# A gated graph network followed by graph attention: another order of the work ahead of the first block

## The chip, the cores and the metric

The kernel runs on one core of a Trainium2 chip. The core has five engines that run side by side, each working through its own list of instructions in order and waiting on semaphores for the others: TensorE (PE in the profile, with weight loads shown as PEld), VectorE (DVE), ScalarE (ACT), GpSimd (POOL) and SyncE (SP, which here only issues transfers). The metric is the device time of one execution in microseconds, lower is better; the figure for a kernel is the median of its runs.

## The reference

There are 64 graphs of 256 nodes with 256 features. Layer 0 is a gated graph network of three steps with one recurrent cell, layer 1 is graph attention. Each adds its result to its input and normalises.

```
A = (adj != 0)
h = x
for i in range(3):
    m = einsum('bnd,de->bne', h, weight[i])
    aggr = einsum('bst,bsd->btd', A, m)
    h = gru_cell(aggr, h, w_ih, w_hh, b_ih, b_hh)
x = layernorm(x + h)

Wh = x @ W;  s1 = Wh @ a[:256];  s2 = Wh @ a[256:]
e = leaky_relu(s1[:, :, None] + s2[:, None, :], 0.2)
attn = softmax(where(adj > 0, e, -9e15), axis=2)
out = layernorm(x + attn @ Wh)
```

## The kernel before

Two graphs form a pair, and there are 32 pairs. A pair goes through three recurrent blocks (one for each layer i of the network), then through its attention. The blocks of different pairs are interleaved: (0,0), (1,0), (0,1), (2,0), (1,1) and so on, so that the side work of one block lies beside the matmuls of another. "(p,i)" stands for block i of pair p in what follows.

The weight of a step is folded into the input weight of the cell: since aggr @ w_ih.T = (A.T h) weight[i] w_ih.T, the kernel forms weight[i] w_ih.T once for each i ("fold", L234) and aggregates h itself (L439). The large products are made in a reduced format from three pieces of each factor: an upper piece H (ScalarE, L132), a lower piece L (L135, or L149 for weights) and a cross piece D (L138). So `hH`, `hL`, `hD` are the pieces of the state, `aH`, `aL`, `aD` those of the aggregate, `whhH/L/D` and `wc0H/L/D` to `wc2H/L/D` those of the weights. `cut_weight` (L140) makes the three pieces of a weight out of a PSUM bank: upper on ScalarE, a remainder `cut` on VectorE, its scaling on GpSimd (L149), the cross piece on VectorE. While the program's clock is negative, the remainder's buffer is one of three of the tag "n"; afterwards it is the single buffer "wh".

A block's `gates` (L456) runs four products for each of the two halves e of the state: r (6 pairs of matmuls on two PSUM banks, `pga` and `pgb`), n (3 pairs on the state alone), z (6), t (3 on the aggregate alone). All of them are line L468. An evacuation (L473, L475, L477), a nonlinearity (L486) and blending (L494 to L507) follow each product on ScalarE, VectorE and GpSimd.

The order of the work is written out by hand. `at(t, step)` and `after(dt, step)` put a step into a heap by its tick; `tick()` advances the program's clock and emits all steps that are due, those of one tick in the order in which they were entered. `gates` calls `tick()` between parts of its products. Ticks order instructions when the program is built; they are not time on the chip. `front` (L385) enters the preparation of a block with a `pace`: ticks of turning x to the transposed state (L280), its split into `hi` and `lo` (L405, L135), aggregation (L439), pieces of the aggregate, and in a second tuple the pieces hH, hL, hD of the state.

Eight PSUM banks serve everything (`bank`, L106). A new bank is one whose earlier reader has been emitted, so a matmul that opens a bank waits for the engine that reads that earlier content.

Ahead of block (0,0) the kernel turns w_ih (`rows_inp`, tiles `rows_aH`, `rows_aL`) and w_hh (`rows_hid`, tiles `rows_hH`, `rows_hL`) on TensorE (L219), cuts w_hh, folds weight[0] (`square_T` at L222 turns it, L238 multiplies), makes the 0/1 matrix A of the first pair (`ones`, L380), and aggregates. The folds of weight[1] and weight[2] and `attention_rows` (L242) are entered for later ticks and are emitted inside the first blocks. `attention_rows` forms two extra columns of W, W a1 and W a2 (L247, copied by L249), and takes the column means off (a tile `mean` filled with 1/256 at L251, the matmul L254, the subtraction L256); the results are used only much later, by the first attention (L589).

Of the kernel before, what the change touches and what calls it, by code (L numbers as in the profile page):

```python
# [9 lines left out]
F32 = mybir.dt.float32  # L10
# [9 lines left out]
P = 128  # L20
# [7 lines left out]
def kernel(  # L28
# [37 lines left out]
    nc = tc.nc  # L66
    B, N, D = x.shape
# [25 lines left out]
    def after(dt, step):  # L93
        at(clock[0] + dt, step)
# [5 lines left out]
    def tick(n=1):  # L100
        for _ in range(n):
            clock[0] += 1
            run_due()


    def bank(name):  # L106
        return psum.tile([P, 512], F32, tag="bank", name=name)
# [3 lines left out]
    def evacuate(dst, src):  # L111
        copies[0] += 1
        if copies[0] % 2:
            nc.scalar.copy(dst, src)
        else:
            nc.vector.tensor_copy(dst, src)
# [55 lines left out]
    def load_adj(p):  # L172
        if p < NP:
            a_sb = loaded_adj[p] = io.tile([P, G, C, N], I32, tag="adj", name=f"adj_{p}")
            nc.sync.dma_start(a_sb, adj[p * G:(p + 1) * G].rearrange("g (c p) n -> p g c n", p=P))
# [34 lines left out]
    def wih(e, o0, o1):  # L210

        return (wihT if o1 <= 512 else wihT2)[:, e, o0 % 512:o0 % 512 + o1 - o0]

    def rows_T(src, use):
        o0, o1, t = src
        for c in range(C):
            pt = bank("pw")
            for o in range(o1 - o0):
                nc.tensor.transpose(pt[:, o * P:(o + 1) * P], t[:, o, c * P:(c + 1) * P], ident)  # L219
            use(c, o0 * P, o1 * P, pt[:, :(o1 - o0) * P])  # L220

    def square_T(src, name):  # L222
        pt = bank("pw")
        for e in range(C):
            for d in range(C):
                nc.tensor.transpose(pt[:, (e * C + d) * P:(e * C + d + 1) * P],
                                    src[:, d, e * P:(e + 1) * P], ident)
        dst = work.tile([P, GN], F32, tag="z", name=name)
        nc.scalar.copy(dst, pt)
        return dst.rearrange("p (e d) -> p e d", e=C)  # L230
# [3 lines left out]
    def fold(i, wT, d, parts=PARTS):  # L234
        for o0, o1 in parts:
            pt = bank("pw")
            for e in range(C):
                nc.tensor.matmul(pt[:, :o1 - o0], wT[:, e, d * P:(d + 1) * P], wih(e, o0, o1),  # L238
                                 start=(e == 0), stop=(e == C - 1))
            cut_weight([t[:, d, o0:o1] for t in wc[i]], pt[:, :o1 - o0], f"{i}_{d}_{o0}")  # L240

    def attention_rows():  # L242
        gwT = square_T(gw, "gwT")
        for d in range(C):
            pt = bank("pw")
            for f in range(C):
                nc.tensor.matmul(pt[:, :2], gwT[:, f, d * P:(d + 1) * P], a_w[:, :, f],  # L247
                                 start=(f == 0), stop=(f == C - 1))
            nc.vector.tensor_copy(gw[:, d, D:], pt[:, :2])  # L249
        mean = late.tile([P, C, GN], F32, tag="vT", name="mean")[:, 0, :P]  # L250
        nc.vector.memset(mean, 1.0 / D)  # L251
        pt = bank("pw")[:, :D + 2]
        for d in range(C):
            nc.tensor.matmul(pt, mean, gw[:, d, :], start=(d == 0), stop=(d == C - 1))  # L254
        for d in range(C):
            nc.vector.tensor_sub(gw[:, d, :], gw[:, d, :], pt)  # L256


    class Pair:
# [112 lines left out]
    def begin(p):  # L372
        s = pairs.setdefault(p, Pair())
        s.hT = work.tile([P, C, GN], F32, tag="hT", name=f"hT_{p}", bufs=4)

    def ones(p):
        s = pairs[p]
        s.adj = loaded_adj.pop(p)
        s.A = work.tile([P, G, C, N], F32R, tag="A", name=f"A_{p}", bufs=3)
        nc.vector.tensor_scalar(s.A, s.adj, 0.0, None, op0=ALU.not_equal)  # L380
# [469 lines left out]
    def rows_hid(part):  # L850
        rows_T(part, lambda c, o0, o1, pt: cut_weight([t[:, c, o0:o1] for t in whh], pt, f"h{c}_{o0}"))

    def rows_inp(part):
        rows_T(part, lambda c, o0, o1, pt: evacuate(wih(c, o0, o1), pt))
    begin(0)
    take_x(0)
    front(0, 0, clock[0] + 1, ((0, 1, 2, 9, 11, 12), (7, 8, 13)))
    tick(2)
    rows_inp(wi_n[0])
    tick()  # L860
    rows_hid(wh_n[0])
    tick()
    rows_inp(wi_n[1])
    tick()
    rows_hid(wh_n[1])
    wT = square_T(w_n[0], "wT_0")
    nc.vector.tensor_add(b_sum, bi, bh)
    tick()
    ones(0)
    load_adj(1)  # L870
    tick()
    for parts in PARTS:
        for d in range(C):
            fold(0, wT, d, (parts,))
            tick(2)
    tick(10)
    load_x(1)
    clock[0] = 0
    wTs = {}

    def start_fold(i):
        wTs[i] = square_T(w_n[i], f"wT_{i}")
    for i in range(1, L):
        after(8 * i - 7, lambda i=i: start_fold(i))
        for d in range(C):
            after(8 * i - 5 + 3 * d, lambda i=i, d=d: fold(i, wTs[i], d))
    after(8 * L - 7, attention_rows)

    for n, (p, i) in enumerate(blocks):
        if n + 1 < len(blocks):  # L890
# [59 lines left out]
```

## Time and profile before

| what | value |
|---|---|
| median of three runs | 2091.16 us (2088.38 to 2096.8) |
| the profiled execution | 2091.86 us |
| its span, first to last instruction | 2090.0 us |
| TensorE busy in the span | 2052.3 us (98%) |
| TensorE busy in 0 to 28 us | 17.55 us |
| TensorE busy in 28 to 62 us | 34.00 us |
| TensorE busy in 62 to 78 us | 13.27 us, granted clock 0.89 |
| TensorE busy in 78 to 178 us | 100.00 us, granted clock 1.00 |
| mean granted clock over the span | 0.996 |

The profile page gives the busy time of each engine, and the chain of waits that ended last. Other views of the same trace give the busy time in any stretch, the instructions in order of time with the idle time ahead of each and what ended it, and the waits of one engine summed by what ended them. "Busy" for TensorE contains a modelled end of each matmul, so start-to-start distances are the better measure of its pace.

### The profile page before, as it was taken

To read this page: it belongs to the slowest core of one execution; us is meant where nothing else is said; L and a number is where in the kernel's file an instruction comes from. 1 tells how busy PE (TensorE), PEld (TensorE's weight loads), DVE (VectorE), ACT (ScalarE), POOL (GpSimd) and SP (SyncE) were. 2 spreads that over 40 slices of the span, in tenths; PEclk is the share of its full clock that TensorE was granted. 3 is DMA by queue.
4 is the path that set the end of the run, shared out by engine and by line. 5 is a ranking of instruction groups with operands and counts; after the bars stand their busy time and mean duration, and the time that the engine had idled before them with its cause. 6 is when DMAs were issued, how large, how long until landed. Compare 5 with 4: busy or idle time off the path is not lost.

```text
span 2090.0 us, 31381 instructions
## 1 busy us (share of the span) xinstructions
PE 2052.3 (98%) x9892; PEld 1726.0 (83%) x9892; DVE 1780.5 (85%) x2886; ACT 1655.3 (79%) x3015; POOL 1604.8 (77%) x1114
## 2 busy tenths in 40 slices
PE   8999999999999999999999999999999999999996
PEld 5788888888888888888888888888888888888885
DVE  5666778898888899888998988998888998988887
ACT  4566787888887888888888887888888888888775
POOL 6777777777877787878777877787878787878763
PEclk9999999999999999999999999999999999999998
DMA  4111235665666665665665666665766665666321
GB/s 131 31 41 41 72 88 114 141 141 117 136 138 135 141 137 121 136 136 137 140 136 124 136 137 137 137 138 123 134 138 139 134 141 123 138 136 137 61 61 61
DMA packets 531621, 247.98 MB, mean 119 GB/s; under 512 B 359616, under 2 KB 523200, under 8 KB 531456
## 3 DMA queue, kind: packets, MB, share of 16 engines
q1 hardware_dynamic: 529664, 244.14, 53.1%
q8 instruction: 79, 1.29, 0.3%
q10 hardware_dynamic: 1616, 1.57, 0.2%
q14 instruction: 86, 0.70, 0.1%
q0 software_dynamic: 176, 0.27, 0.1%
HBM read 69.74 MB, written 33.55 MB: 49 GB/s over the span
## 4 chain that ended last, share of the span: by engine, by line
PE 89%; DVE 3%; ACT 3%; issue 2%; POOL 1%; DMA 1%; SPq 0%; POOLq 0%; ACTq 0%; DVEq 0%
PE pga L468 46%; PE pgb L468 23%; PE pa L439 8%; PE pwh L589 5%; PE po L673 5%; DVE lo L135 1%; PE s L608 1%; PE pt L369 1%; ACT sc L636 1%; DMA rows_hH<-in_L_gnn_w_hh_dram 0%; PE po L796 0%; ACT L636 0%; PE pw L238 0%; ACT n L475 0%; DMA second<-v 0%
## 5 line engine op out<-in xcount | busy, mean ns | idle before, releaser
L494 POOL TENSOR_TENSOR t<-hT,n 128x512 f32<-128x512 f32 x192 | 263.0, 1370 | 191.6 <-ACT n L486 191.3
L500 POOL TENSOR_TENSOR n<-n,r 128x512 f32<-128x512 f32 x192 | 316.5, 1648 | 81.8 <-ACT r L486 42.6
L504 POOL TENSOR_TENSOR n<-n,t 128x512 f32<-128x512 f32 x192 | 282.7, 1472 | 122.7 <-DVE t L477 116.0
L468 PE MATMUL pga<-hH,whhH_whh 128*128 128x512 f32 x1152 | 370.5, 403 | 0.0
L468 PE MATMUL pgb<-hD,whhD_whh 128*128 128x512 f32 x1152 | 356.8, 391 | 1.4 <-DVE hD L138 1.4
L468 PE MATMUL pga<-hL,whhL_whh 128*128 128x512 f32 x1152 | 356.7, 391 | 0.4 <-POOL hL L135 0.4
L495 POOL TENSOR_TENSOR t<-t,z 128x512 f32<-128x512 f32 x192 | 271.4, 1414 | 15.1
L135 POOL TENSOR_TENSOR hL<-hT,hH 128x1024 fp32r<-128x1024 f32 x96 | 255.5, 2661 | 9.0 <-ACT hH L132 9.0
L468 PEld LDWEIGHTS pgb<-hD,whhD_whh 128*128 128x128 f32 x1152 | 216.2, 188 | 49.2 <-DVE hD L138 1.7
L468 PEld LDWEIGHTS pga<-hL,whhL_whh 128*128 128x128 f32 x1152 | 216.2, 188 | 47.8 <-POOL hL L135 0.8
L468 PEld LDWEIGHTS pga<-hH,whhH_whh 128*128 128x128 f32 x1152 | 207.5, 188 | 34.1
L473 ACT ACTIVATE r<-pga 128x512 f32<-128x512 f32 x192 | 114.1, 594 | 109.1 <-PE pga L468 79.6
L439 PE MATMUL pa<-A,lo 128*128 128x256 f32 x768 | 192.5, 283 | 6.1 <-DVE lo L135 6.1
L138 DVE SCALAR_TENSOR_TENSOR hD<-hH,hT 128x1024 fp32r<-128x1024 f32 x96 | 195.7, 2039 | 0.0
L439 PE MATMUL pa<-A,hi 128*128 128x256 f32 x768 | 194.2, 285 | 0.2 <-DVE A L380 0.2
L477 DVE SCALAR_TENSOR_TENSOR r<-pgb,r 128x512 f32<-128x512 f32 x192 | 132.0, 687 | 68.9 <-PE pgb L468 43.4
L486 ACT ACTIVATE n<-n,bi 128x512 f32<-128x512 f32 x192 | 139.1, 724 | 64.0 <-POOL n L504 63.8
L507 DVE TENSOR_TENSOR hT<-t,n 128x512 f32<-128x512 f32 x192 | 185.0, 963 | 0.0
L135 DVE TENSOR_TENSOR aL<-pa,aH 128x512 fp32r<-128x512 f32 x192 | 130.9, 682 | 56.6 <-ACT aH L132 56.5
L473 ACT ACTIVATE t<-pga 128x512 f32<-128x512 f32 x192 | 115.1, 600 | 71.1 <-PE pga L468 66.0
L132 ACT ACTIVATE aH<-pa 128x512 fp32r<-128x512 f32 x192 | 115.8, 604 | 64.0 <-PE pa L439 64.0
L439 PEld LDWEIGHTS pa<-A,lo 128*128 128x128 f32 x768 | 146.4, 191 | 13.8 <-DVE lo L135 7.6
(172 smaller groups left out, 5405.9 us busy)
## 6 DMA issues: line engine op xcount, KB each, us to landing
adj<-in_adj_dram SPq DMA_DIRECT2D x64, 512.0 KB, 3.8
second_h<-first_h SPq DMA_DIRECT2D x204, 128.0 KB, 4.2
x<-in_x_dram SPq DMA_DIRECT2D x32, 512.0 KB, 3.8
xT<-hT SPq DMA_DIRECT2D x32, 512.0 KB, 4.5
vT<-xT SPq DMA_DIRECT2D x32, 512.0 KB, 3.3
second<-v SPq DMA_DIRECT2D x116, 128.0 KB, 3.8
sc<-eT SPq DMA_DIRECT2D x232, 64.0 KB, 2.3
out_dram<-eT SPq DMA_DIRECT2D x29, 512.0 KB, 4.3
```

The lines of the kernel that those rows point to most:

```text
L135: eng.tensor_sub(dst, src, hi.bitcast(F32))
L138: nc.vector.scalar_tensor_tensor(dst, hi.bitcast(F32), 1.0 + U, src, op0=ALU.mult, op1=ALU.subtract)
L439: nc.tensor.matmul(pt[:, g * N:(g + 1) * N], h[:, g * C + c, :], s.A[:, g, c, :], start=(n == 0), stop=(n == len(todo) - 1))
L468: nc.tensor.matmul(pt, w[:, d, o * P:(o + 1) * P], m[:, d, :], start=n in (0, ends + 1), stop=n in (ends, len(todo) - 1))
L473: nc.scalar.activation(dst, a, AF.Copy, scale=1.0 + U)
L477: nc.vector.scalar_tensor_tensor(dst, b, -1.0 / U, dst, op0=ALU.mult, op1=ALU.add)
L486: nc.scalar.activation(dst, dst, func, bias=bias)
L494: nc.gpsimd.tensor_sub(t, h, n)
L495: nc.gpsimd.tensor_mul(t, t, z)
L500: after(2, lambda r=r, n=n: nc.gpsimd.tensor_mul(n, n, r))
L504: after(1, lambda n=n, t=t: nc.gpsimd.tensor_add(n, n, t))
L507: after(lags[2], lambda n=n, t=t, h=h: nc.vector.tensor_add(h, t, n))
```

## The change

It touches only what is emitted ahead of block (0,0) and what is entered there for later ticks.

- The opening sequence, before written as calls with `tick()` between them, is entered with `after`, and the preparation of block (0,0) gets another pace: both halves of x are split one tick earlier, and the pieces of the state are due at 5, 6 and 10 in place of 7, 8 and 13. In the order that is built, the two `lo` subtractions come first on VectorE, the four transposes of `rows_hL` come ahead of the four of `rows_aL` on TensorE, hL comes ahead of wc0L on GpSimd, and hD comes ahead of aL and aD on VectorE, with the four 256-wide cut instructions of weight[0] behind them.
- What is still pending when the first block begins is carried over with its remaining ticks.
- The fold of weight[1] starts at tick 0, and both its halves are due at tick 3 (before: ticks 3 and 6). The fold of weight[2] starts at 7, its halves are due at 12 and 16 (before 9, 11 and 14).
- `attention_rows` becomes four steps, at ticks 17, 18, 21 and 21: turn W, multiply by a, form the mean, subtract (before: all in one, at tick 17).

Every instruction of the kernel before is still there, with the same shapes. Behind block (1,0) and the first few instructions of (0,1) the order on every engine is that of before; the order of the transfers on SP is the same throughout. Line numbers in the changed kernel lie 9 higher from `Pair` on.

```diff
-    def attention_rows():
-        gwT = square_T(gw, "gwT")
+    rows_of = {}
+
+    def rows_turned():
+        rows_of["T"] = square_T(gw, "gwT")
+
+    def rows_times():
         for d in range(C):
-            pt = bank("pw")
+            pt = rows_of[d] = bank("pw")
             for f in range(C):
-                nc.tensor.matmul(pt[:, :2], gwT[:, f, d * P:(d + 1) * P], a_w[:, :, f],
+                nc.tensor.matmul(pt[:, :2], rows_of["T"][:, f, d * P:(d + 1) * P], a_w[:, :, f],
                                  start=(f == 0), stop=(f == C - 1))
             nc.vector.tensor_copy(gw[:, d, D:], pt[:, :2])
-        mean = late.tile([P, C, GN], F32, tag="vT", name="mean")[:, 0, :P]
+
+    def rows_mean():
+        mean = rows_of["mean"] = late.tile([P, C, GN], F32, tag="vT", name="mean")[:, 0, :P]
         nc.vector.memset(mean, 1.0 / D)
-        pt = bank("pw")[:, :D + 2]
+        pt = rows_of["m"] = bank("pw")[:, :D + 2]
         for d in range(C):
             nc.tensor.matmul(pt, mean, gw[:, d, :], start=(d == 0), stop=(d == C - 1))
+
+    def rows_less():
         for d in range(C):
-            nc.vector.tensor_sub(gw[:, d, :], gw[:, d, :], pt)
+            nc.vector.tensor_sub(gw[:, d, :], gw[:, d, :], rows_of["m"])
+    attention_rows = rows_turned, rows_times, rows_mean, rows_less
...
+    wTs = {}
     begin(0)
     take_x(0)
-    front(0, 0, clock[0] + 1, ((0, 1, 2, 9, 11, 12), (7, 8, 13)))
-    tick(2)
-    rows_inp(wi_n[0])
-    tick()
-    rows_hid(wh_n[0])
-    tick()
-    rows_inp(wi_n[1])
-    tick()
-    rows_hid(wh_n[1])
-    wT = square_T(w_n[0], "wT_0")
-    nc.vector.tensor_add(b_sum, bi, bh)
-    tick()
-    ones(0)
-    load_adj(1)
-    tick()
-    for parts in PARTS:
+    front(0, 0, clock[0] + 1, ((0, 0, 1, 9, 11, 12), (5, 6, 10)))
+    for n, part in enumerate(wi_n):
+        after((3, 5)[n], lambda part=part: rows_inp(part))
+    for n, part in enumerate(wh_n):
+        after((4, 4)[n], lambda part=part: rows_hid(part))
+    after(5, lambda: wTs.update({0: square_T(w_n[0], "wT_0")}))
+    after(5, lambda: nc.vector.tensor_add(b_sum, bi, bh))
+    after(5, lambda: ones(0))
+    after(5, lambda: load_adj(1))
+    for n, o in enumerate(PARTS):
         for d in range(C):
-            fold(0, wT, d, (parts,))
-            tick(2)
-    tick(10)
-    load_x(1)
+            after((7, 14)[n] + 2 * d, lambda o=o, d=d: fold(0, wTs[0], d, (o,)))
+    after(17, lambda: load_x(1))
+    tick(25)
+    while pending and pending[0][0] <= clock[0]:
+        run_due()
+    moved = [(t - clock[0], n, step) for t, n, step in pending]
+    pending[:] = sorted(moved)
     clock[0] = 0
-    wTs = {}
 
     def start_fold(i):
         wTs[i] = square_T(w_n[i], f"wT_{i}")
-    for i in range(1, L):
-        after(8 * i - 7, lambda i=i: start_fold(i))
-        for d in range(C):
-            after(8 * i - 5 + 3 * d, lambda i=i, d=d: fold(i, wTs[i], d))
-    after(8 * L - 7, attention_rows)
+    for i, (t0, t1, t2) in enumerate(((0, 3, 3), (7, 12, 16)), 1):
+        after(t0, lambda i=i: start_fold(i))
+        after(t1, lambda i=i: fold(i, wTs[i], 0))
+        after(t2, lambda i=i: fold(i, wTs[i], 1))
+    for t0, step in zip((17, 18, 21, 21), attention_rows):
+        after(t0, step)
```

## The prediction

> **What bounds the kernel now.** I began with the page's first part: TensorE is busy for 98% of the span, so the question is where its idle 37.7 us lie and which of them the change can reach. The waits of TensorE in the first 80 us give them with the time before each instruction and what ended it:
>
> ```profile
> span 2090.0 us, 31381 instructions
> PE 2052.3 (98%) x9892; PEld 1726.0 (83%) x9892; DVE 1780.5 (85%) x2886; ACT 1655.3 (79%) x3015; POOL 1604.8 (77%) x1114
> ...
> PE pt L280 <- DMA x<-in_x_dram: 6.0, 1, 6.0
> PE pw L247 <- ACT gwT L229: 2.3, 1, 2.3
> PE pw L219 <- DMA rows_hH<-in_L_gnn_w_hh_dram: 1.4, 1, 1.4
> PE pgb L468 <- DVE hD L138: 1.4, 1, 1.4
> PE pw L238 <- ACT wT L229: 0.7, 1, 0.7
> PE pw L254 <- DVE mean L251: 0.4, 1, 0.4
> PE pga L468 <- POOL hL L135: 0.4, 1, 0.4
> PE pga L468 <- DVE aL L135: 0.3, 1, 0.3
> PE pa L439 <- DVE A L380: 0.2, 1, 0.2
> ```
>
> 6.0 and 1.4 us are first transfers, which stay. The rest is two spots: 0.2 + 0.4 + 0.3 + 1.4 = 2.3 us in the first r product (18 to 28 us), and 2.7 us around `attention_rows` (62 to 67 us). From 78 us on TensorE is never idle for 100 us, and the built order there is unchanged: what is won ahead of it is kept.
>
> The chain of waits from 60 us shows why the second spot exists, and the busy table by stretch what follows it (columns: stretch, length, busy us of PE, PEld, DVE, ACT, POOL, then granted clock):
>
> ```profile
> 62.01 1.28 POOL t L494
> 63.37 1.27 POOL t L495
> 64.66 0.59 ACT gwT L229
> 65.30 1.07 PE pw L247 x8
> 66.53 0.18 DVE mean L251
> 66.75 1.44 PE pw L254 x4
> ...
> 68.00:69.00 1.00, 1.00 (x6) 1.00 (x5) 0.78 (x3) 0.00 (x0) 0.00 (x0) 0.50 0.00 0
> 69.00:70.00 1.00, 1.00 (x4) 0.81 (x3) 0.89 (x2) 0.59 (x1) 0.00 (x0) 0.50 0.00 0
> ```
>
> The copy of the turned W (gwT) takes a buffer of the tag "z" and waits for GpSimd's blend; TensorE waits for the copy, and then runs at half clock from 68 to nearly 71 us. The last two views are the order in time on GpSimd and VectorE, and the transfers (last column: us from issue to landing):
>
> ```profile
> 25.54 1.46 DVE L138 SCALAR_TENSOR_TENSOR hD<-hH,hT 128x1024 fp32r<-128x1024 f32 x1
> 73.42 2.40 POOL L135 TENSOR_TENSOR hL<-hT,hH 128x1024 fp32r<-128x1024 f32 x1 [7.57 <-ACT hH L132]
> 73.62 3.29 DVE L138 SCALAR_TENSOR_TENSOR hD<-hH,hT 128x1024 fp32r<-128x1024 f32 x1
> ...
> rows_hL<-in_L_gnn_w_hh_dram SPq DMA_DIRECT2D x1, 256.0 KB, 10.7
> ```
>
> hD took 1.46 us at first and 3.29 us where GpSimd's hL had started 0.20 us ahead of it: it seems to stand still until hL ends at 75.82.
>
> **What the Trainium skill says.** "TensorE: Matmul & The Clock Gate", Part 1, says that TensorE falls to half its clock after an idle window of about 3.4 us and needs a busy window to recover. The trace agrees in kind: granted clock 0.50 behind waits of 2.34 and 0.39 us that lie close together, and no loss behind the single wait of 1.41 us at 25.6 us (1.00). "PSUM — Partial Sum Buffer", Engine vs sequencer instructions, says that the queues of ScalarE, VectorE and GpSimd are strictly first in, first out; every row of the trace that I read is in that order, and the new wait below rests on it. "GPSIMD Engine Reference", Specifications, says that GpSimd shares its memory interface with VectorE where VectorE has two inputs from SBUF; the 3.29 us agree.
>
> **Part 1, the opening.** `rows_hL` now comes ahead of `rows_aL` on TensorE. It was issued at 1.79 us and landed 10.7 us later, 12.49; TensorE is at that place at 11.95, so it waits until 12.61, where it also stood before, but four transposes of `rows_aL` (0.115 us each start to start) now come behind. Transposes of weight[0] go from 13.07 to 13.53, end at 13.98; the copy wT follows at 14.15, takes 0.59, and the fold starts at 14.80 in place of 14.35: **0.45 us lost**.
>
> From there by before's start-to-start times, in the new order: fold of the first part 3.70 us, to 18.50; aggregation 16 x 0.119 = 1.90, to 20.40 (A is ready at 17.2, since `lo` no longer stands ahead of it: no wait); fold of the second part 1.54, to 21.94; hH, hL, aH 3 x 0.46, to 23.32; the four transposes of weight[1] 0.36, to 23.68; aL, hD, aD 3 x 0.46, to 25.06. Do the others deliver? GpSimd: hL starts when the last piece of w_hh ends, 18.05, and takes 2.37, ready at 20.42 for 22.4; two wc0L of 1.49 (0.06 between) are done at 22.0 and 23.55, and the second is needed at 23.91. VectorE: the second wc0 cut can start at 19.3, its two instructions end at 20.5 (0.60 apart), hD takes 1.46, to 21.95, needed at 24.1; aL, aD, aL, aD at 0.60 end at 24.35, the last needed at 24.83. Before, this point was at 28.10. **Won: 3.04 us** net of the 0.45. Of it 2.31 is the waits; the rest is restart, e.g. 0.57 and 0.58 us from hL and hD to the next where 0.46 is usual. Margins of 0.4 to 0.5 us are thin, and GpSimd's is the thinnest.
>
> **Part 2, the folds.** From 28.10 to 52.90 TensorE had no wait; its work there is the same sum of 24.80 us in another order, so it gains nothing. It can lose: both halves of fold 1 now go through the single "wh" buffer in a row, and z, t, the aggregation of (1,0) and the next r open banks that these cuts hold. First ScalarE piece at about 29.4; then cut 0.70, GpSimd 1.50, cut 0.42, GpSimd 0.85, cut 0.70, GpSimd 1.50, cut 0.42 and cross 0.33, with 0.05 to 0.1 between: the four banks come free at about 30.9, 32.5, 34.5 and 36.2 us. TensorE opens their successors at about 34.4 (pgb of z), 35.3 (t), 36.7 (aggregation) and 37.6 (r). Slack 1.4 us at least: **0**. The transposed x of pair 1 is evacuated behind those cuts, at 36.2 + 0.6 + 0.6 = 37.4, and is read at about 40 or later. Fold 2's second half lies inside z of (1,0) and needs banks free at 50.9 and 52.7 (needed from 55.2).
>
> SP's queue keeps its order: the next adj starts when A is done (17.2, before 18.23), x of pair 1 behind it at 17.7, and with the 5.1 us of the slowest x it lands by 22.8, needed at 25.1. x of pair 2 waits for the second `lo` of pair 1, which moves behind fold 1's cuts on GpSimd (36.8 to 38.1, before 36.23 to 37.52); it is needed near 77.
>
> **Part 3, attention_rows.** Before, from the turning of W (62.37) to the end of t (71.17) took 8.80 us. The same items without waits and at full clock: turning 0.36, eight a_w rows about 0.9, mean four rows of 0.215 = 0.86 (by the fold of layer 1, 2.58 us for six times 256 columns, so 0.43 for each of the two products), transposes of h 0.36, t 1.38: 3.86. **Won: 4.94**, if the copy gwT is hidden: it now has the transposes of h and t, 1.7 us, between it and its reader; it is ready by 60.3, needed at 61.3. The copies to gw follow at 62.5, and `mean` needs them much later.
>
> But the fill of `mean` (0.18) is now behind hD, aL, aD and r's evacuation on VectorE. With the transposes of h's second half ending at P, the sequence of before gives: hi at P + 0.28, hH 0.48 later, released to both engines, GpSimd first by 0.20 as before, hD through 3.29 us, then 3 x 0.60 and the fill: P + 7.3. TensorE has r, two aggregations and n in between (71.52 to 77.67 before, 6.15 us). **A new wait of about 1.2 us**; behind it on TensorE stand z, t and block (0,1), behind the fill on VectorE the subtraction and the second aL, which before's order had 8 us later. If VectorE got hD in first it is 0; if the fill slips further, 2 at most, as nothing longer stands in front. I take 1.2, since all four instructions stand as before relative to each other.
>
> Sum: 3.04 + 4.94 - 1.2 = 6.8 us. The profiled execution took 2091.86 (span 2090.0 and 1.86 around it), so 2085.1; that execution is 0.7 above the median of the runs: **2084.4 us**, 0.32% less than 2091.16. What a measurement of this kernel can tell from no change is about 0.5%, 10.5 us.
>
> **The rivals.**
> - *No new wait at `mean`.* If hD precedes hL, 8.0 won: 2083.2. For it: at 47.02 hD took 1.24 while GpSimd's t (2.28) gave way. Against it: the same release of both by hH as at 73.4.
> - *The first product still waits, or the clock still drops.* GpSimd's margin of 0.36 or VectorE's 0.48 is used up; all four old waits cannot return, one of up to 1.4 can; or the 1.2 us wait brings half clock for some 3 us of matmuls, 1.5 us. Either: about 5.3 won, 2085.9; both, 2087.3.
> - *More than 10.5 us won.* All waits of the two spots, both restarts and the half clock are in my sum; it would need 4 us that no view shows, or a pair of medians that lie apart (the three runs spread over 8.4 us). About 2080.
> - *Slower.* The serial cuts of fold 1 hold the banks: place, the opening of r's pga near 37.6 us. Their chain of 6.8 us must become at least 8.2 before TensorE waits, and 15.0 before the wait eats the 6.8 won; 2092 and above from there. VectorE idles during GpSimd's part, so nothing on the page stretches it that far.
>
> **How the numbers follow.** Chances: my case 0.46 (own range 2082.5 to 2086.5), no new wait 0.16, less won 0.18, over 10.5 won 0.16, slower 0.04. With the spread of runs, 2079.5 to 2089 holds 8 in 10. Faster by over 0.5%: 0.16; within: 0.80; slower: 0.04.
>
> **What would show it.** In the profile after: the first r product ends at about 25 us with no wait above 0.4; no wait in front of the a_w product and clock 1.00 between 58 and 75; one wait near 69 us of about 1.2 us in front of `mean`, ended by VectorE; z of (1,0)'s second half starts at about 71 in place of 77.67; from there every start is a constant 6 to 7 us earlier. I am wrong if TensorE waits for a bank between 30 and 45 us, or if the shift seen at 80 us isn't there at the end.

## The result and the profile after

| | before | after |
|---|---|---|
| first timing, 9 runs each | 2095.2 us (2088.38 to 2096.8) | 2088.77 us (2085.74 to 2091.97) |
| ratio after/before, 95% interval | | 0.9977 [0.9966, 0.9988] |
| a later timing, 9 and 5 runs | 2089.75 us (2087.95 to 2093.27) | 2081.95 us (2079.95 to 2083.81) |
| ratio, 95% interval | | 0.9965 [0.9951, 0.9979] |
| profiled execution, its span | 2091.86, 2090.0 us | 2089.42, 2087.6 us |

The kernel became 6.4 us faster by the medians of the first timing, 7.8 by those of the later one. The forecast was 2084.4 us, 6.8 below the 2091.16 it started from. So the difference was near and the time was not: the median of either kernel moves by some 7 us from one set of runs to the next (before: 2087.32 to 2095.2 us over five sets). Where that comes from is part of the experiments. Each ratio in what follows is to the runs of before in the same set.

The page's first part and the waits of TensorE in the first 80 us of the kernel after (columns: us in total, times, longest):

```profile
span 2087.6 us, 31381 instructions
PE 2052.9 (98%) x9892; PEld 1727.6 (83%) x9892; DVE 1781.8 (85%) x2886; ACT 1655.2 (79%) x3015; POOL 1605.5 (77%) x1114
```

```profile
PE pt L289 <- DMA x<-in_x_dram: 6.1, 1, 6.1
PE pw L219 <- DMA rows_hH<-in_L_gnn_w_hh_dram: 1.4, 1, 1.4
PE pw L260 <- DVE mean L257: 1.1, 1, 1.1
PE pw L238 <- ACT wT L229: 0.7, 1, 0.7
PE pga L477 <- POOL wc0L_wc L149: 0.5, 1, 0.5
```

The nine waits of before have become five. The copy gwT, hD, hL, aL and A are gone from the list. New are 0.5 us for GpSimd's scaling into wc0L, where the prediction allowed no wait above 0.4; the wait at `mean` grew from 0.4 to 1.1 us, where it expected 1.2.

The busy table by stretch (length, busy us of PE, PEld, DVE, ACT, POOL, granted clock) and the order in time on VectorE and GpSimd show the second spot of the kernel after:

```profile
66.00:68.00 2.00, 2.00 (x14) 1.82 (x13) 2.00 (x3) 1.28 (x3) 1.58 (x1) 1.00 0.00 0
68.00:70.00 2.00, 2.00 (x15) 1.79 (x14) 2.00 (x2) 0.76 (x2) 2.00 (x2) 1.00 0.00 0
70.00:72.00 2.00, 0.85 (x5) 0.41 (x3) 1.83 (x4) 0.92 (x2) 1.17 (x2) 1.00 0.00 0
```

```profile
66.62 3.27 DVE L138 SCALAR_TENSOR_TENSOR hD<-hH,hT 128x1024 fp32r<-128x1024 f32 x1
69.82 0.68 DVE L135 TENSOR_TENSOR aL<-pa,aH 128x512 fp32r<-128x512 f32 x1
70.42 0.67 DVE L138 SCALAR_TENSOR_TENSOR aD<-aH,pa 128x512 fp32r<-128x512 f32 x1
71.01 0.68 DVE L486 SCALAR_TENSOR_TENSOR r<-pgb,r 128x512 f32<-128x512 f32 x1
71.67 0.17 DVE L257 MEMSET mean<- 128x128 f32 x1
...
66.42 2.40 POOL L135 TENSOR_TENSOR hL<-hT,hH 128x1024 fp32r<-128x1024 f32 x1 [1.71 <-ACT hH L132]
```

The half clock of 68 to 71 us is gone. hL starts 0.20 us ahead of hD, hD stands until hL ends and takes 3.27 us, and the fill of `mean` comes last in that queue. This is the sequence that the prediction gave, instruction by instruction.

To compare executions I use four starts that every version has, and count the waits of TensorE for `lo` behind 100 us (explained below). "First fold" is the start of the product at L238; "first r done" is the start of what TensorE does behind the first r product; "W turned" is the start of the transposes of gw; "h5" is the start of the fifth rounding of h (hH on ScalarE). before_again, old_folds, hD_later, warm and warm_all were run once, so that only their profiles are used.

| profile | first fold | first r done | W turned | h5 | waits for lo | span |
|---|---|---|---|---|---|---|
| before | 14.35 | 28.10 | 62.37 | 106.34 | 5 | 2090.0 |
| before_again | 14.48 | 28.24 | 62.51 | 106.48 | 5 | 2089.8 |
| rows_only | 16.30 | 29.40 | 65.17 | 106.81 | 2 | 2086.0 |
| lo_first_before | 15.96 | 29.34 | 64.83 | 108.80 | 0 | 2084.9 |
| after | 15.66 | 26.87 | 61.06 | 101.63 | 6 | 2087.6 |
| after_again | 16.44 | 26.82 | 60.99 | 101.58 | 0 | 2079.0 |
| opening_only | 15.53 | 26.72 | 60.99 | 104.91 | 8 | 2094.3 |
| mean_early | 15.66 | 26.86 | 61.04 | 100.22 | 1 | 2077.8 |
| old_folds | 16.30 | 26.68 | 60.93 | 102.55 | 0 | 2079.2 |
| hL_earlier | 15.69 | 26.84 | 61.01 | 100.19 | 0 | 2081.1 |
| lo_first_after | 15.62 | 28.11 | 62.29 | 102.84 | 0 | 2079.6 |
| hD_later | 15.40 | 25.79 | 59.97 | 100.54 | 2 | 2080.7 |
| warm | 14.70 | 26.20 | 60.38 | 100.93 | 3 | 2081.3 |
| warm_all | 14.37 | 26.30 | 60.49 | 101.02 | 4 | 2084.0 |
| best_cold | 15.96 | 26.37 | 60.55 | 99.73 | 1 | 2078.3 |
| best_warm | 16.26 | 28.39 | 62.57 | 101.75 | 2 | 2079.7 |
| lo_first_best | 16.04 | 26.46 | 60.64 | 99.82 | 0 | 2074.8 |

Between the profiles of before and after the opening won 1.23 us (28.10 to 26.87) in place of 3.04. From W's turning to h5 43.97 became 40.57 us: 3.40 won, for 4.94 - 1.2 = 3.74. h5 is 4.7 us earlier and the end of the span 2.4.

### The profile page after: what moved, and what is told of

Its sections match the earlier page's. It is cut to its first block, busy times and chain, and to the rows that moved or that the text cites. A ratio compares the mean times of both kernels' runs of the same rounds, so it can differ in the third digit from the quotient of the medians.

```text
span 2087.6 us, 31381 instructions
## 1 busy us (share of the span) xinstructions
PE 2052.9 (98%) x9892; PEld 1727.6 (83%) x9892; DVE 1781.8 (85%) x2886; ACT 1655.2 (79%) x3015; POOL 1605.5 (77%) x1114
## 3 DMA queue, kind: packets, MB, share of 16 engines
q8 instruction: 79, 1.29, 0.3%
## 4 chain that ended last, share of the span: by engine, by line
PE 92%; DVE 3%; ACT 2%; issue 1%; POOL 1%; DMA 0%; POOLq 0%; ACTq 0%; SPq 0%; DVEq 0%
PE pga L477 47%; PE pgb L477 24%; PE pa L448 8%; PE pwh L598 5%; PE po L682 5%; DVE lo L135 1%; PE pt L378 1%; PE s L617 1%; ACT sc L645 1%; PE pw L238 0%; DMA rows_hH<-in_L_gnn_w_hh_dram 0%; PE po L805 0%; ACT L645 0%; DVE hT L516 0%; PE pwh L742 0%
```

## The experiments

### Both kernels once more

Nothing is edited in `before_again` and `after_again`.

> The kernel before once more, nothing edited, to see what of its opening and of the stretch behind gwT is the kernel's own and what is chance. Theory A (the sum on record): the opening is fixed by the program; the eight transposes into rows_hH take 1.10 us, the first fold starts at 14.35 us, the first r product ends at 28.10 us, the clock drops to half once behind gwT, and the half 2 of z of block (1,0) starts at 77.67 us, all within 0.2 us. Theory B (the clock of TensorE is chosen at fixed steps of 3.41 us whose phase is chance in each execution): the transposes into rows_hH take anything between 1.1 and 2.0 us, the first fold starts up to 1 us earlier or later, and the loss behind gwT (52.90 to 77.67, 24.77 us) may be up to 1.8 us smaller.

> The kernel after once more, nothing edited. Theory A, B and C all read its profile as the program's own: the first fold at 15.4 to 15.7 us, the first r product ends at 26.6 to 26.9, the wait of 1.1 us at mean, the fifth rounded piece of h at 101.3 to 101.7 us. What differs from execution to execution is only the number of waits of 1.2 us for lo after 500 us (5 and 5 in two profiles of before, 6 in one of after). Timed: 4.7 us below before when those waits are equally many, so a ratio of 0.9977 with an interval of 0.001.

`before_again` repeated the profile of before within 0.15 us in every start of the table, which by itself spoke for theory A. `after_again` repeated after within 0.1 us from the first r product to h5; only its fold, at 16.44, came 0.74 us later than expected at the latest, and no wait for wc0L followed. It was the later profiles that spoke for B. The eight transposes into rows_hH, in before, after, and lo_first_before (start, duration):

```profile
11.01 1.10 PE L219 MATMUL pw<-ident,rows_hH 128*128 128x128 f32 x8 [1.42 <-DMA rows_hH<-in_L_gnn_w_hh_dram]
```

```profile
11.11 1.97 PE L219 MATMUL pw<-ident,rows_hH 128*128 128x128 f32 x8 [1.36 <-DMA rows_hH<-in_L_gnn_w_hh_dram]
```

```profile
11.00 1.97 PE L219 MATMUL pw<-ident,rows_hH 128*128 128x128 f32 x8 [1.27 <-DMA rows_hH<-in_L_gnn_w_hh_dram]
```

The same transposes, in kernels whose opening is the same (the first and the third), run at either pace. In after_again they took 1.09 us, and then the granted clock fell to 0.50 in the next stretch (columns as above, with the share and GB/s of the DMA at the end):

```profile
11.00:13.00 2.00, 1.15 (x9) 0.92 (x9) 0.85 (x2) 1.09 (x2) 0.00 (x0) 0.85 1.10 347
13.00:15.00 2.00, 2.00 (x10) 2.00 (x11) 2.00 (x5) 1.14 (x3) 1.71 (x2) 0.50 1.10 377
```

(In the profile of after the same column reads 1.00 from 9 to 17 us although the pace is halved; the first stretch of a trace has no record of the clock, so there the start-to-start distance is what counts.) The Trainium skill, "TensorE: Matmul & The Clock Gate", Part 1, says that the window of about 3.4 us over which the activity is judged runs free and does not start with the kernel, so that the point of transition differs from run to run. The traces agree: the fold of the old opening starts at 14.35, 14.48, 15.96 or 16.30, that of the new one anywhere from 15.40 to 16.44.

The phase itself can be read. The records of the clock last 3.41 us or a multiple of it (in before, half clock for 3.41 us from 67.45; in best_warm, below, for 6.83 us from 12.97), so one can count back in steps of 3.41 us from where a record begins. In before TensorE was busy for the whole step from 6.01 to 9.42 us, and the record of full clock begins at 9.42. In after the steps lie otherwise: from 3.94, 7.35 and 10.77 us TensorE was busy for 1.25, 2.40 and 3.07 us, and full clock begins only behind the third, at 14.18. In the fourteen profiles without added transposes it begins at 9.00 to 9.63 us in five and at 13.88 to 15.57 in nine.

A good phase is not enough for the new opening. after_again, old_folds and lo_first_after had full clock by 9.63 us and lost it at 12.42, 12.61 and 13.04, behind a step with 1.44 to 1.59 us of work; before and before_again had 1.93 and 1.75 us of work there and kept it. The new order empties that step: TensorE now waits 0.4 to 0.7 us for the transfer of `rows_hL`, where the old order had the transposes of `rows_aL`. No edit tests this by itself, and warm (below) kept its clock behind 1.46 us, so the amount of work that is enough stays open. But in none of the ten profiles of the new opening without added transposes does the fold start before 15.40.

What follows for the change: the old opening pays for a bad phase in full, and once more when its wait of 1.2 us for hD brings half clock from 29 to 32 us. W is turned at 62.37, 62.51, 64.83 and 65.17, mean 63.72. With the new opening and hD at its place (after, after_again, opening_only, mean_early, old_folds, hL_earlier, lo_first_after) it is turned at 60.93 to 61.06 in six of seven profiles and at 62.29 in one, mean 61.19. That is 2.5 us won on average of these few profiles, and 1.3 between the profiles of before and after, where before had a good phase and after a bad one.

### Parts of the change alone

`opening_only` keeps the new opening, `rows_only` the four steps; the rest is as before. `old_folds` is the kernel after with the old ticks of the folds. The core of the edits:

```diff
 # opening_only
-    for t0, step in zip((17, 18, 21, 21), attention_rows):
+    for t0, step in zip((17, 17, 17, 17), attention_rows):
 # opening_only, rows_only and old_folds
-    for i, (t0, t1, t2) in enumerate(((0, 3, 3), (7, 12, 16)), 1):
-        after(t0, lambda i=i: start_fold(i))
...
+    for i in range(1, L):
+        after(8 * i - 7, lambda i=i: start_fold(i))
+        for d in range(C):
+            after(8 * i - 5 + 3 * d, lambda i=i, d=d: fold(i, wTs[i], d))
```

> The change's new opening alone: folds of layers 1 and 2 at their old ticks and the four steps on gw's extra columns together at one tick, as before. Markers: start of the first fold, end of the first r product, start of r of (1,0), half 2 of z of (1,0), and the fifth rounded piece of h on ScalarE (106.34 us before, 101.63 after). Theory A (record): everything is 3.04 us earlier than before from the first r product on, so that marker lies at 103.3, and the kernel is 3.0 us faster. Theory B (the opening is worth only 1.2 us, for hD on VectorE holds back GpSimd's scalings into wc0L and the transposes run at half pace when the clock's phase is unlucky): first fold between 14.8 and 15.7, the first wc0L of 512 columns takes 2.2 to 2.4 us instead of 1.49, a wait of about 0.5 us before the product of the first block that needs wc0L, the first r product ends between 26.0 and 26.9, the marker lies at 104.2 to 105.2, and 1.2 to 2.1 us are won. Both: the wait before a_w (2.0 us and more) and the half clock after it are still there.

> The kernel before with only the four steps on gw's extra columns set at ticks 17, 18, 21 and 21 (old opening, old ticks of the folds). Theory A (record): the wait for gwT ahead of the products with a_w and the half clock behind it go (4.94 us), a wait of about 1.2 us before the products with mean comes, since the fill of mean stands behind hD on VectorE: 3.7 us won, the marker of the fifth h piece at 102.6. Theory B says the same of this part, with the loss before depending on the phase of the clock: 2.0 to 3.7 won. Rival: with the old folds' ticks the steps meet fold 1 or fold 2 on the banks or the cuts and win less than 2.

> The kernel after with the folds of layers 1 and 2 back at their old ticks. Theory A (record: the new ticks cost and win nothing): every marker as in after, the fifth rounded piece of h at 101.4 to 101.8 us. Theory E (from rows_only, where the wait before a_w was 0.53 and not gone: the old ticks put the cut of fold 2 on GpSimd so late that the buffer of gwT is still held by GpSimd's blend): a wait of 0.4 to 0.6 us before a_w, no other change, the marker at 102.3 to 102.8 us, so that the new ticks are worth 0.8 to 1.1 us.

Measured: opening_only 2088.39 us (14 runs), ratio 0.9988 [0.9977, 0.9999]; h5 at 104.91, so 1.4 to 1.6 us won as B expected, with the wait of 2.3 us for gwT still there. (By time it is 3.0 us, which A had, but the interval reaches from 0.2 to 4.8 us; h5 is what tells A from B.) rows_only 2088.78 us (21 runs), ratio 0.9989 [0.9980, 0.9998]; from W's turning to h5 41.64 us, 2.3 won and not 3.4. Its opening fell on a bad phase, so that h5 itself, at 106.81, is no earlier than in before and misses the 102.6 expected. old_folds explains the missing 1.1. Its waits from 20 to 80 us, and GpSimd's order there:

```profile
PE pw L260 <- DVE mean L257: 1.2, 1, 1.2
PE pw L251 <- ACT gwT L229: 0.5, 1, 0.5
```

```profile
57.60 1.49 POOL L149 TENSOR_SCALAR wc2L_wc<-cut 128x512 fp32r<-128x512 f32 x1 [0.72 <-DVE cut L135]
59.64 0.85 POOL L149 TENSOR_SCALAR wc2L_wc<-cut 128x256 fp32r<-128x256 f32 x1 [0.54 <-DVE cut L135]
60.57 1.28 POOL L503 TENSOR_TENSOR t<-hT,n 128x512 f32<-128x512 f32 x1
61.93 1.29 POOL L504 TENSOR_TENSOR t<-t,z 128x512 f32<-128x512 f32 x1
```

With the old ticks the scalings of fold 2's second half stand ahead of the blend whose end gives the buffer of gwT free (61.93 + 1.29); the copy starts at 63.25 instead of 61.63 and TensorE waits. With the new ticks they stand behind it. h5 is at 102.55 instead of 101.58: theory E holds, and the new ticks are worth 1.0 us. The steps of h5 are thus 1.5 for the opening (mean of the two profiles of before less opening_only), 2.4 for the four steps, 1.0 for the folds.

### The two waits of the kernel after

```diff
 # mean_early: in rows_turned (tick 17) in place of rows_mean (tick 21)
+        rows_of["mean"] = late.tile([P, C, GN], F32, tag="vT", name="mean")[:, 0, :P]
+        nc.vector.memset(rows_of["mean"], 1.0 / D)
 # hD_later
-    front(0, 0, clock[0] + 1, ((0, 0, 1, 9, 11, 12), (5, 6, 10)))
+    front(0, 0, clock[0] + 1, ((0, 0, 1, 9, 11, 12), (5, 6, 13)))
```

> The kernel after with one edit: mean is taken and filled in the step that turns gw (tick 17), not in the third step (tick 21), so that its fill stands ahead of hD on VectorE. Theory A and B alike: the wait of 1.15 us before the products with mean goes, half 2 of z of (1,0) starts 1.1 us earlier than in the kernel after (against r of (1,0), 21.35 us there, 20.2 here), and that stays to the end: 1.1 us faster than the kernel after, 4.2 to 7.5 faster than before. Rival: the fill was only the last of several things that came late (the copies into gw's columns, or the sub of hL from GpSimd), and less than 0.5 us goes.

> The kernel after with hD of the first block set at tick 13 of its front in place of 10, so that VectorE forms it behind both halves of aL and aD and not beside the first scalings into wc0L on GpSimd. Theory B (GpSimd's scaling of 512 columns took 2.35 us in place of 1.49 because the two-input hD, 1.31 us, ran beside it): both scalings take 1.5 us, the second ends near 24.6, the wait of 0.53 us before the product with wc0L goes and no wait for hD above 0.2 us takes its place; the first r product ends at 25.9 to 26.0 us in place of 26.87, with the first fold at 15.66 as there. Theory A's margin seen as GpSimd's own spread, nothing to do with hD: the scaling stays at 2.2 to 2.4 us and the end at 26.8, or at 27 and later since hD is now late.

mean_early: the wait is gone, TensorE is busy without a break from 62 to 78 us, and from W's turning to h5 it takes 39.18 us, 1.4 less than after (1.1 was expected; the wait was 1.15). 2081.75 us (6 runs), ratio 0.9963 [0.9949, 0.9978], which by time can't be told from after_again's 0.9965. The fill was what came last, nothing else.

hD_later: the opening. In the kernel after, hD on VectorE, the first scaling on GpSimd and the product that waits (start, duration):

```profile
21.30 1.31 DVE L138 SCALAR_TENSOR_TENSOR hD<-hH,hT 128x1024 fp32r<-128x1024 f32 x1
21.61 2.35 POOL L149 TENSOR_SCALAR wc0L_wc<-cut 128x512 fp32r<-128x512 f32 x1
25.59 0.50 PE L477 MATMUL pga<-aL,wc0L_wc 128*128 128x512 f32 x1 [0.53 <-POOL wc0L_wc L149]
```

And with hD at tick 13:

```profile
21.38 3.06 POOL L149 TENSOR_SCALAR wc0L_wc<-cut 128x512 fp32r<-128x512 f32 x2
23.44 1.22 DVE L138 SCALAR_TENSOR_TENSOR hD<-hH,hT 128x1024 fp32r<-128x1024 f32 x1
```

The scaling starts 0.31 us behind hD and ends 0.86 later than its 1.49 us would have it, about the 0.93 us for which hD still ran (21.61 to 22.54, where the next starts on VectorE). In hD_later both scalings take 3.06 us together, although hD lies beside the second for a microsecond: there hD started second, and neither was longer. From the first fold to the end of the first r product it is 10.39 us in place of 11.21, so 0.82 won. Theory B holds for this half of it.

### TensorE kept busy

```diff
     make_identity(nc, ident)
+    def keep_busy(n):
+        pt = psum.tile([P, 512], F32, tag="bank", name="keep")
+        for k in range(n):
+            nc.tensor.transpose(pt[:, k % 4 * P:(k % 4 + 1) * P], ident, ident)
+    keep_busy(20)
...
+    after(4, lambda: keep_busy(10))
```

> The kernel after with 20 transposes of the identity ahead of the transposes of x and 10 between those of rows_aH and rows_hH, so that TensorE is busy from about 1.5 us on; nothing reads what they make. Theory C (the first fold is 0.86 us later than on record because the transposes of rows_hH and rows_hL ran at half clock: 1.76 and 0.85 us in place of 0.94 and 0.46): the eight transposes into rows_hH take about 1.1 us, the wait for rows_hL's transfer at about 12.6 us comes back, the first fold starts at 14.7 to 14.9 in place of 15.66, and the first r product ends at 25.9 to 26.1 us, the wait for wc0L still there. Rival (the first fold is late for another reason, the order of rows_hL and rows_aL or the copy wT): the fold stays at 15.5 or later. If the clock does not rise by these transposes, nothing moves or the opening is up to 1 us later.

> The busy TensorE and hD at tick 13 together, and rows_aL ahead of rows_hL again. Theories B and C together: first fold 14.3 to 14.5 us (14.80 less the 0.45 us that the wait for rows_hL cost on record), the first r product ends at 24.6 to 25.1 us: the 3.04 us on record and up to 0.45 more. Rival (the two losses share a cause, or a third instruction becomes late): 25.5 us or later, with a wait of 0.4 us or more that names it.

> The same with TensorE kept busy from 1.4 us on by transposes of the identity (20 and 10, read by nobody). In warm_all hD started at 22.40 us, just ahead of the second scaling into wc0L, and held it for 0.9 us; here, with rows_hL again ahead of rows_aL, hD should start at about 22.75 us and the second scaling at 22.5. If so: both scalings take 1.5 us, the first fold starts at 14.7, the first r product ends at 25.1 to 25.4 us (25.06 on record), the fifth rounded piece of h at 98.4 to 98.9 us. If hD comes in first again (a matter of 0.25 us): the scaling takes 2.4 us, the product ends at 26.2, and the marker is 99.5.

warm_all has hD at tick 13 besides, and rows_aL ahead of rows_hL (ticks 4 and 5 for the two parts of w_hh in place of 4 and 4); best_warm is mean_early with hD at tick 13 and the lines above.

In warm the transposes took 1.09 us, TensorE waited 0.5 us for rows_hL, and the first fold started at 14.70, all as C said and as the prediction had it (14.80). But the first r product ended at 26.20, 0.67 us earlier for a fold 0.96 us earlier: the wait for wc0L grew from 0.5 to 0.8 us. In warm_all the fold came at 14.37, the wait grew to 1.2 us and the end stayed at 26.30, where 24.6 to 25.1 was expected; it is the rival's case. hD started at 22.40 there, just ahead of the second scaling.

GpSimd's chain (four pieces of w_hh, hL, two scalings) starts between 13.00 and 13.74 us in every new opening, hardly moved by TensorE, and where the fold is early it holds the end of the first r product near 26 to 27 us. So six of seven new openings end within 0.2 us of each other although their folds start 0.9 us apart: the four with a fold at 15.53 to 15.69 waited 0.5 us for wc0L. The two with a fold at 16.30 and 16.44 had no such wait and came to the same time without it.

In best_warm the transposes of the identity were over at 8.97 us, two waits of 1.9 and 0.9 us for transfers followed, and the clock was halved from 12.97 to 19.79 us: product at 28.39, h5 at 101.75, the expectation missed by 3 us. In warm full clock was kept over waits of 2.0 and 0.5 us. So TensorE kept busy ahead of a wait carries its clock over that wait in one execution and not in another; it is not a safe gain.

### What spreads the runs

The spans differ by up to 9 us where the starts from the first r product to h5 agree within 0.1 (after and after_again). The waits of TensorE behind 110 us differ by more than 0.6 us in one line only, shown here for before and after:

```profile
PE pa L439 <- DVE lo L135: 6.1, 5, 1.2
```

```profile
PE pa L448 <- DVE lo L135: 7.3, 6, 1.2
```

In after_again there is none; 8.6 us of span for six waits is 1.43 us each. With 1.43 us taken off for each wait, h5 and the end of the span lie 1975.0 to 1978.0 us apart in sixteen of the seventeen profiles (hL_earlier, below: 1980.9); without that, 1975.0 to 1989.4. VectorE and GpSimd of the kernel before, at a place where TensorE waits and one pair of graphs later where it doesn't:

```profile
628.00 2.93 DVE L135 TENSOR_TENSOR lo<-V,hi 128x512 fp32r<-128x512 f32 x1
628.00 2.38 POOL L135 TENSOR_TENSOR hL<-hT,hH 128x1024 fp32r<-128x1024 f32 x1
...
691.85 0.68 DVE L135 TENSOR_TENSOR lo<-V,hi 128x512 fp32r<-128x512 f32 x1
691.85 2.94 POOL L135 TENSOR_TENSOR hL<-hT,hH 128x1024 fp32r<-128x1024 f32 x1
```

Both start in the same hundredth of a microsecond, and one of the two stands until the other is nearly done: either lo takes 2.93 us, or hL takes 0.56 more and nobody waits. In each of the profiles of before, after and after_again there are 25 such meetings, all within 10 ns; lo loses 5, 6 and 0 of them. Which of the two got in first can't be seen at this distance (the recorded order doesn't sort the cases), so I infer it from hD behind hL above and from the edit below that sets lo ahead. The Trainium skill, "GPSIMD Engine Reference", Specifications, says that GpSimd shares its memory interface with VectorE's instructions that have two inputs from SBUF; lo is one, and the longer times agree. Two edits take the meeting away, hL_earlier on GpSimd and lo_first on VectorE, where lo comes one tick earlier and so ahead of the evacuation of t:

```diff
 # hL_earlier (on mean_early)
-    THIRD = (2, 3, 4, 7, 8, 9), (3, 6, 7)
+    THIRD = (2, 3, 4, 7, 8, 9), (3, 5, 7)
 # lo_first, on before, on after and on best_cold
-                at(e + dt[2] + (2, 4)[i] * d + n, lambda step=step, d=d: step(d))
+                at(e + dt[2] + (2, 4)[i] * d + n - 1 * (i == 1 and d == 1 and n == 2), lambda step=step, d=d: step(d))
```

> The kernel with the early fill of mean and one more edit, far from the change: in the fronts of the third layer GpSimd's hL is set at tick 5, not 6, ahead of the blend n and not behind it. Theory D (runs of one kernel differ by 8 us because VectorE's lo and GpSimd's hL start in the same instant once in every pair of graphs, and where GpSimd gets in first lo takes 2.93 us in place of 0.68 and TensorE waits 1.22 us, restart included about 1.5): the starts lie apart, waits before the aggregation for lo of 1.2 us go (5 in the kernel before, 6 in after, 1 in mean_early) or come in every pair; where they go, the times of the runs lie within about 2 us, near 2078 us. Rival (the spread has another source): runs still spread over 6 us and more, median near 2081.75.

> The kernel before with one edit, outside the change: on VectorE the piece lo of the second half of h for the third layer is formed ahead of the evacuation of t and not behind it, so that it is under way before GpSimd's hL can start. Theory D (each wait for lo costs 1.43 us, since GpSimd got in first, and their number, 0 to 8, is chance): no wait for lo is left, the fifth rounded piece of h still starts at 106.3 to 106.5 us, the runs lie within 3 us of each other at 2083.5 to 2085.5 us (2090.0 less 5 times 1.43, and 1.8 around the span). Rival (the waits come at another place, or t now comes late): a time at or above the 2090 to 2095 of before and a spread of 6 us or more.

> The same edit in the kernel after. If D holds, the two kernels with the edit show the change without the chance waits: the marker of the fifth h piece at 101.5 to 101.7 us, runs within 3 us of each other at 2079.5 to 2081.5 us, 4 to 5 us less than the other with the edit (the shift of the marker is 4.8). Theory A (record): 6.8 us less. If the change also makes chance waits rarer, the difference in time was larger without the edit (6.4 and 7.8 us in two sets of runs) than it is here.

hL_earlier (hL ahead of the blend on GpSimd in the third layer's fronts): no wait for lo, 18 runs within 3.7 us (2082.22 to 2085.92), where the 22 runs of before beside them spread over 11.25. The spread went as D said; the median of 2083.75 us, ratio 0.9975 [0.9967, 0.9983], did not fall to the 2078 expected. Against the profile of mean_early it loses about 4 us in small steps from 500 us to the end; lo takes 1.70 us there, and where those steps lie is open.

lo_first_before: 2086.42 us (13 runs, 2084.34 to 2087.57), ratio 0.9993 [0.9985, 1.0002]. lo_first_after: 2079.55 us (5 runs, 2077.93 to 2081.44), ratio to before 0.9963 [0.9951, 0.9976]. lo now starts 0.34 us ahead of hL and takes 0.93:

```profile
630.14 0.93 DVE L135 TENSOR_TENSOR lo<-V,hi 128x512 fp32r<-128x512 f32 x1 [0.18 <-ACT hi L329]
630.48 2.86 POOL L135 TENSOR_TENSOR hL<-hT,hH 128x1024 fp32r<-128x1024 f32 x1
```

No wait for lo is left in either, and their 13 and 5 runs spread over 3.2 and 3.5 us, where the 17 runs of before beside them spread over 6.2 (35 in another set over 12.4). With the profiles above, D holds for the waits and the spread.

D's time for lo_first_before, 2083.5 to 2085.5 us, was missed by 0.9: the edit won 0.9 us, not 7. The runs of before beside it were already at 2087.32, so by 1.43 us a wait they had, as an estimate, about two waits and not the five of the first profile (2091.86 us). Of the 2.9 us that two waits would give 0.9 was measured; the profile of lo_first_before has a bad phase (below), but whether most of its runs had one isn't shown. What makes the waits more frequent in one set than in another (medians of before 2095.2, 2091.4, 2088.95, 2089.75 and 2087.32 us; the last four sets ran on four different chips) is open.

Without the waits the two medians lie 6.9 us apart, more than the 4.8 that I expected from h5: these two profiles have h5 5.96 us apart, and from there to the last one every rounding of h is 5.8 to 6.2 us earlier (5.3 at the end of the span). h5 itself, at 108.80 and 102.84, lies 2.4 and 1.2 us later than I expected: both openings fell on a bad phase, which is about as much as the runs still spread. There is no sign that the change makes the waits for lo rarer: 6.4 and 7.8 us with them, 6.9 without.

### A faster version

> The kernel after with the two edits that each won by themselves: the fill of mean in the step that turns gw, and hD of the first block at tick 13. If they add: the first r product ends at 25.8 to 26.1 us, no wait at wc0L and none at mean, the fifth rounded piece of h at 99.1 to 99.5 us (106.34 before), so 2.1 to 2.4 us less than after and about 7 us less than before, the number of waits for lo being equal. Rival (the early fill needs VectorE where hD now is, or a third wait appears): 100.0 us or later.

> The same edit in the kernel with the early fill of mean and hD at tick 13. If all three add: no wait at mean, none for lo, the marker at 98.9 to 99.8 us, runs at 2077.5 to 2079.5 us, 1.8 to 2.7 us below the kernel after with the same edit and some 11 below before. Rival: 0 to 1 us below it, the gain given back later.

best_cold is mean_early with hD at tick 13, lo_first_best the same with the edit at lo. best_cold has no wait from 12 us to 500 us other than 0.7 us for wT; h5 at 99.73, 1.9 us ahead of after, 0.2 us later than expected; its phase was a bad one (fold at 15.96). 2080.18 us (5 runs), ratio 0.9962 [0.9949, 0.9975]; best_warm 2081.49 us, 0.9962 [0.9949, 0.9974]. By time neither can be told from after. lo_first_best: h5 at 99.82, 2076.64 us (5 runs, 2076.6 to 2078.45), ratio 0.9953 [0.9940, 0.9967]. That is 2.9 us below lo_first_after, a little more than the 1.8 to 2.7 expected, with five runs each that just overlap. It is the lowest median of the study.

## Why the prediction was right or wrong

- **"Won: 3.04 us", the opening: the term that was mis-sized.** It was 1.23 us in the profiles of before and after, and a mean of 2.5 us at W's turning over four and seven profiles. Two durations in it failed, and they make up the 1.81 us between the two profiles. "Two wc0L of 1.49 ... done at 22.0 and 23.55": the first took 2.35 us behind hD, GpSimd's chain ended near 25.5, and the margin called the thinnest was spent. From the fold to the end of the product it took 11.21 us for 10.26, so 0.95 lost, and hD_later takes 0.82 of it back. And the fold "starts at 14.80": it came at 15.66, 0.86 later. It needs the transposes of rows_hH at 0.115 us each, which the profile of before showed in a good phase of the clock; after had 0.23, and warm, with the quick pace, started at 14.70. The shared interface stood in the prediction and was used for hD behind hL, but not for the scaling behind hD. The rival "the first product still waits" named this margin, and this is the case that came.
- **"Slack 1.4 us at least: 0", the folds.** Right for the banks: TensorE has no wait between 27 and 62 us. But the folds' ticks decide when gwT can be copied, and by old_folds that is 1.0 us of what part 3 counted as its own.
- **"Won: 4.94", less "a new wait of about 1.2 us".** The mechanism was right. Measured 3.40 for 3.74, the wait 1.15 us (1.1 in the list above) with hL first by 0.20 and hD at 3.27; clock 1.00 from 62 to 78 us. Without the wait, in mean_early, 4.79 of the 4.94 is won, so the fill costs 1.4 us, its wait and a little more.
- **"2084.4", the time itself: the base failed.** It rested on three runs and one profile, whose five waits for lo and good phase of the opening are chance. The first timing put the same kernel at 2095.2 us, another at 2087.32. In the first timing 4.0 of the 4.4 us between 2084.4 and 2088.77 are the base (2091.16 against 2095.2). That the difference of 6.8 us came out near (6.4, 7.8, and 6.9 without the chance waits) is in part luck: the sum was 1.8 us too high for the opening it was written for, and the old opening is on average slower than the profile that the sum began with.
- **"A constant 6 to 7 us earlier".** It was 4.7 us up to 500 us in the profiles of before and after, then changed by the waits for lo, and 2.4 at the end of the span; in the pair without these waits 5.8 to 6.2 up to the last rounding of h, and 5.3 at the end.

## What to carry to other kernels

When a view shows one engine standing still behind another on the shared memory interface, go through every place where a moved instruction newly starts beside one of that other engine, above all where the margin is under a microsecond. Before a sum of a few microseconds is set against one profiled execution, look for what varies between executions of the same kernel: two starts in the same hundredth of a microsecond, and matmuls early in the program whose pace depends on the clock's phase. And an instruction that needs nothing but a free buffer, such as a fill, belongs ahead of the queue that it would otherwise stand behind.

## What the runs showed of the hardware

- Of two instructions on VectorE and GpSimd that met in these traces, the one that started second stood: hD 3.27 us behind hL (1.22 in hD_later), the one-input scaling 2.35 in place of 1.49 behind hD; where lo and hL start within 10 ns, either can be the one (lo 2.93 for 0.68, or hL 2.94 for 2.38). 0.34 us of lead were enough to turn it round, though not free: lo then took 0.93 (lo_first_before). hD begun within a scaling was not longer (1.22).
- With thirty transposes into a bank that nobody reads, full clock began at 4.12, 7.32 and 6.14 us (warm, warm_all, best_warm) against 9.00 to 15.57 in the fourteen other profiles. In best_warm waits of 1.9 and 0.9 us halved it again from 12.97 to 19.79; in warm waits of 2.0 and 0.5 did not.
